# Message products of two batches at once by Strassen's form, with block sums made by accumulating DMAs

## The chip, the cores and the metric

The kernel runs on one core of a Trainium2 chip. The metric is device time in microseconds (us) of that core; lower is better. Five engines run side by side, each through its own list of instructions in order: TensorE (PE, matmuls into PSUM), VectorE (DVE), ScalarE (ACT), GpSimd (POOL) and SyncE (SP, which only issues DMAs). An engine whose next instruction must wait holds up everything behind it in its own list.

## The reference

Two layers work on `x` of 16 batches x 1024 nodes x 128 features with one symmetric 0/1 matrix `adj` of 1024 x 1024.

```python
x = layernorm(x + attention(x, adj))      # layer 0, once per batch
h = x                                     # layer 1: five steps of a gated unit
for _ in range(5):
    m  = adj @ h                          # the message product; m_in and m_out are the same here
    z  = sigmoid([m, m] @ w3.T + b3 + h @ u3.T + c3)
    r  = sigmoid([m, m] @ w4.T + b4 + h @ u3.T + c3)
    hv = tanh([m, m] @ w5.T + b5 + (r * h) @ u5.T + c5)
    h  = (1 - z) * h + z * hv
out = layernorm(x + h)
```

Because both adjacency inputs are `adj`, `[m, m] @ w.T` is `m @ (wa + wb).T`; the kernel adds the two halves of each weight once. The tests of the inputs that let the kernel use a short form of the softmax end in a flag; a slower general program stands behind it and is not run here.

## The kernel before

**Data.** `h` is kept in two layouts: `hT` (features on the 128 partitions, 1024 nodes along them) for the gates, and, as weights of the message product, `hN` (nodes on partitions, in 8 chunks of 128). `adj` stays in SBUF as `float32r`[...]; the weights side is split into two `float32r` numbers (high part and rest, `split`, L501 and following) so that two matmuls give the product of a float32 by a 0/1 matrix. A message product of one batch and one step is therefore 2 halves of the nodes x 8 chunks x 2 parts = 32 matmuls of 128 x 512 (L895). The gates (L926, L936, L952, L953) use plain float32 matmuls, ten per batch and step.

**One step of one batch.** The 32 message matmuls go into two PSUM banks; ScalarE copies each to `m` (L913). For each half: `h @ u3` (L926), copied by ScalarE into a second bank (L929) so that both gates can add onto it, two gate matmuls (L936), two tanh (L939), `r*h` on VectorE (L946), two matmuls (L952, L953), tanh (L956), three VectorE instructions that write `hT` (L963, L970, L977). Then the new `h` is turned into `hN`: VectorE transposes 32 x 32 blocks (`T`, L494), four DMAs write the result to a DRAM tile `D` with the blocks in swapped places (L499), one DMA reads it back (`F`, L503), ScalarE writes the high part (L513) and VectorE the rest (L517).

**Layer 0** of each batch (`layer0`) has 32 more matmuls of the same kind (L766), some float32 ones, softmax sums on VectorE, two such turns through DRAM and a layernorm whose power is taken on GpSimd (L463 to L466).

**The order.** Nothing is scheduled by hand. `Plan` takes every piece of work with an engine, a length, a rank and what it reads and writes, plays the engines forward with these lengths and assumed delays, and at each free engine takes the ready piece of lowest rank; buffers have to be free. The instructions are emitted in that order. `rank_of(b, s)` is `5*b + 3*s`, so some three batches are in flight at once, and the last three are spread out to end together. `D` holds offsets from that rank for each kind of work. The delay that the planner assumes between a turned block's read and its use is 2.3 us after the issue.

**DMA queues.** SP issues all DMAs but four of the start. Each of the DMA semaphores is waited for before it is used again; a read of `D` waits on SP for the four writes to land.

Of the kernel before, what the change touches and what calls it, by code (L numbers as in the profile page):

```python
# [26 lines left out]
TINY = 1e-30  # L27
IDLE = 24
# [101 lines left out]
def kernel(  # L130
# [51 lines left out]

# [15 lines left out]
    b5 = const.tile([P, 1], F32, tag="b5", name="b5")  # L198
    ident = const.tile([P, P], F32, tag="ident", name="ident")
# [3 lines left out]
    zeros = const.tile([P, HALF], F32, tag="zeros", name="zeros")  # L203
# [7 lines left out]
    def exact(pools):  # L211

        def pool(name, bufs, space=None):
# [4 lines left out]
        adj = table.tile([P, NC, N], F32R, tag="adj", name="adj")  # L218
        cnt = table.tile([P, NC], F32, tag="cnt", name="cnt")
# [5 lines left out]
            "hl": (2, [P, 2, NC, P], F32R, None),  # L225
            "yT": (1, [P, N], F32, None),
            "part": (1, [P, HALF], F32, None),
            "junk": (1, [P, HALF], F32, None),
            "y0": (4, [P, NC, P], F32, None),
            "hN": (4, [P, 2, NC, P], F32R, None),  # L230
            "hT": (4, [P, N], F32, None),
            "T": (3, [P, HALF], F32, None),
            "F": (3, [P, HALF], F32, None),
            "m": (4, [P, HALF], F32, None),
# [3 lines left out]
            "o": (2, [P, NC, P], F32, None),  # L238
            "look": (2, [P, HALF], F32, None),
# [9 lines left out]
            "D": (6, [P, HALF], F32, bass.MemoryType.DRAM),  # L249
            "ud": (2, [3, N], F32, bass.MemoryType.DRAM),  # L250
# [42 lines left out]
        D = dict(m=0, pu=0, u=0, pr=0.2, pz=0.2, sr=0.3, r=0.3, pv=0.4, sz=0.5, z=0.5, hv=0.6, h=0.6, tr=0.6, split=0.8)  # L293
        D.update(o=3, ln=3.5, out=4, l1=-7, l2=-6, l3=-5, l4=-4, l5=-3, l6=-2.5, l7=-2, l8=-1)

# [3 lines left out]

        def rank_of(b, s):  # L300

            if b < B - 3:
                return 5 * b + 3 * s
            begin = 5 * b - 2 * (b - B + 3)
            end = 5 * B + 4 - 2 * (B - 1 - b)
            return begin + (end - begin) * s / 4


        boot = ("hl", "boot")
        cols = {"wot": slice(0, 128), "a": slice(128, 130), "ws": slice(256, 384), "w345": slice(384, 1152)}  # L310

        def W(name):
            return T(boot, F32, [P, 2 * N])[:, cols[name]]

        ws = ("T", "ws")
        staged = [("hN", "boot", k) for k in range(NC // 2)]
        x0 = ("xt", 0)

        def adj_half(k, e):
            hs = slice(e * HALF, (e + 1) * HALF)  # L320
            rows = adj_t[2 * k * P : 2 * (k + 1) * P, hs].rearrange("(c p) n -> p c n", p=P)
            return T(staged[k], F32, [P, 2, N])[:, :, hs], rows

        def early_loads():
# [28 lines left out]
            writes=[(boot, "early"), (ws, "early"), (x0, "early"), (("xt", 1), "early"), *((t, "early") for t in staged)],  # L353
# [7 lines left out]
        lands(8, [(staged[0], 0)])  # L361
        lands(1, [(("wo",), 0)])
        for k in range(1, NC // 2):
            lands(8, [(staged[k], 0)])
        for k in range(NC // 2):
            lands(8, [(staged[k], 1)])
# [3 lines left out]
        def constants():  # L370
            make_identity(nc, ident)
            nc.gpsimd.memset(shift, -SHIFT)
            nc.gpsimd.memset(ones, 1.0)
            nc.gpsimd.memset(mhalf, -0.5)
            nc.gpsimd.memset(zeros, 0.0)
# [31 lines left out]
        def fill_(k):  # L407
            nc.tensor.matmul(T(("gz", "fill", k)), ident, zeros, start=True, stop=True)
# [10 lines left out]
        def sums():  # L419
            w = W("w345").rearrange("p (j t e) -> p j t e", j=3, t=2)  # L420
            nc.vector.tensor_tensor(wm, w[:, :, 0, :], w[:, :, 1, :], ALU.add)
            nc.vector.tensor_tensor(b5, bias[:, 2:3], bias[:, 4:5], ALU.add)
            nc.vector.tensor_scalar(u5h, u5, 0.5, None, ALU.mult)
# [10 lines left out]
        def adj_tables(c):  # L434
            st = staged[c // 2]

            def left(copy):
                copy(adj[:, c, 0:HALF], T(st)[:, c % 2, 0:HALF])

            def right():  # L440
                nc.scalar.activation(
                    adj[:, c, HALF:N], T(st)[:, c % 2, HALF:N], AF.Identity, accum_out=cnt[:, c : c + 1]
                )

            if c < 4:
                dve(420, -60, lambda: left(nc.vector.tensor_copy), reads=[(st, 0)], writes=[(("A",), c, 0)])
            else:
                act(A, -60, lambda: left(nc.scalar.copy), reads=[(st, 0)], writes=[(("A",), c, 0)])
            act(640, -50, right, reads=[(st, 1)], writes=[(("A",), c, 1)])


        def layernorm(key, g, rank, after, src, dst, write):
# [8 lines left out]
            def power():  # L461
# [3 lines left out]
                nc.gpsimd.tensor_scalar(r[:, 1, :], mean, -1.0, None, ALU.mult)  # L465
                nc.gpsimd.tensor_tensor(r[:, 1, :], r[:, 1, :], r[:, 0, :], ALU.mult)  # L466
# [21 lines left out]
        def flip(name, src, read, dst, write, rank):  # L488


            t, d = ("T", *name), ("D", *name)

            def turn():
                nc.vector.transpose(T(t).rearrange("p (b c i) -> p b c i", b=4, c=4), turned(src()))  # L494

            def away():
                swapped = T(d).rearrange("(b i) (a x) -> a i b x", b=4, a=4)
# [3 lines left out]
            dve(V, rank, turn, reads=read, writes=[(t, 0)])  # L501
            sp(1830, rank, away, reads=[(t, 0)], writes=[(d, 0)], lag=1500)
            sp(450, rank, lambda: nc.sync.dma_start(dst(), T(d)), reads=[(d, 0)], writes=[write], lag=2300)  # L503

        def split(b, s, g, src, read, rank):

            n = ("hN", b, s)
            gs = slice(4 * g, 4 * g + 4)

            def half(k):  # L510
                return T(n)[:, k, gs, :].rearrange("p c (a j) -> p c a j", a=4)

            act(A, rank, lambda: nc.scalar.copy(half(0), src()), reads=read, writes=[(n, g, 0)])  # L513
# [4 lines left out]
                reads=[*read, (n, g, 0)],  # L518
                writes=[(n, g, 1)],
            )  # L520


        def layer0(b):

            first = rank_of(b, 0) - (60 if b == 0 else 0)
# [4 lines left out]
            q, zs, rz, yT, y0, hT = ("q", b), ("zs", b), ("rz", b), ("yT", b), ("y0", b), ("hT", b)  # L530
# [3 lines left out]
            for g in range(4):  # L534
                ph = ("ps", "g", b, "ph", g)

                def ph_(g=g, ph=ph):
                    for j in range(2):
# [13 lines left out]
                pe(460, rank, ph_, reads=[(xt, g // 2), (("wo",), 1)], writes=[(ph, 0)])  # L552
# [135 lines left out]
            rank = rank_of(b, 0) + D["l2"]  # L688
            junk = ("junk", b)
            for c in range(NC):  # L690

                st = staged[c // 2]

                def z_(c=c, st=st):
                    nc.vector.scalar_tensor_tensor(  # L695
                        T(junk),
                        T(st)[:, c % 2, 0:HALF] if b == 0 else adj[:, c, 0:HALF].bitcast(F32),
# [36 lines left out]
            rank = rank_of(b, 0) + D["l3"]  # L734
            size = 1 if b == 0 else 4
            for w in range(2):
                hl = ("hl", b, w)
                for c0 in range(0, NC, size):
                    cs = range(c0, c0 + size)

                    def hi_(w=w, cs=cs, hl=hl):
                        for c in cs:
                            nc.scalar.activation(
                                T(hl)[:, 0, c, :], T(hx)[:, c, 0:P], AF.Copy, scale=T(rz)[:, w, c : c + 1]
                            )

                    def lo_(w=w, cs=cs, hl=hl):
                        for c in cs:
                            nc.vector.scalar_tensor_tensor(  # L749
                                T(hl)[:, 1, c, :],  # L750
                                T(hx)[:, c, 0:P],
                                T(rz)[:, w, c : c + 1],
                                T(hl)[:, 0, c, :].bitcast(F32),
# [5 lines left out]
                    act(1250 * size / 4, rank, hi_, reads=r, writes=[(hl, c, 0) for c in cs])  # L759
                    dve(1050 * size / 4, rank, lo_, reads=[*r, *((hl, c, 0) for c in cs)], writes=[(hl, c, 1) for c in cs])  # L760

            def product(po, w, cs, hs, first, last):
                hl = T(("hl", b, w))
                terms = [(k, c) for c in cs for k in range(2)]
                for i, (k, c) in enumerate(terms):
                    nc.tensor.matmul(  # L766
                        T(po),
                        hl[:, k, c, :],
                        adj[:, c, hs],
                        start=(first and i == 0),  # L770
                        stop=(last and i == len(terms) - 1),
                    )

            rank = rank_of(b, 0) + D["l4"]
            left = slice(0, HALF)
            right = slice(HALF, N)
            for g in range(2):
                po = ("ps", "acc", b, "po", g)
                part = (yT, "p") if g == 0 else (("part", b), "p")

                def part_(g=g, po=po, part=part):
                    dst = T(yT)[:, left] if g == 0 else T(part[0])
                    nc.vector.tensor_tensor(dst, T(po), pairs()[:, g, :], ALU.mult)

                for c0 in range(4 * g, 4 * g + 4, size):
                    cs = range(c0, c0 + size)

                    def po_(g=g, po=po, cs=cs):
                        product(po, 0, cs, left, cs[0] == 4 * g, cs[-1] == 4 * g + 3)
# [5 lines left out]
                        reads=[*((("hl", b, 0), c, k) for c in cs for k in range(2)), *((("A",), c, 0) for c in cs)],  # L795
# [4 lines left out]
            def add_():  # L800
                nc.vector.tensor_tensor(T(yT)[:, left], T(yT)[:, left], T(("part", b)), ALU.add)

            dve(V, rank, add_, reads=[(yT, "p"), (("part", b), "p")], writes=[(yT, "s")])
# [5 lines left out]
                reads=[(xt, 0), (("wsi",), 0)],  # L809
# [5 lines left out]
                lambda: nc.vector.tensor_tensor(T(yT)[:, left], T(px), T(yT)[:, left], ALU.add),  # L815
# [541 lines left out]
```

## Time and profile before

| | |
|---|---|
| Median of 3 runs | 1521.95 us (1521.3 to 1523.5) |
| The profiled execution | 1525.58 us, its span 1523.8 us |
| PE busy | 1496.8 us (98%), 5204 instructions |
| PE weight loads busy | 947.5 us (62%) |
| DVE busy | 988.6 us (65%) |
| ACT busy | 824.4 us (54%) |
| POOL busy | 146.3 us (10%) |
| DMA on the main queue | 142.78 MB, 32.9% of the 16 engines' time |
| Granted TensorE clock | 0.99 of full |

The span runs from the first to the last instruction; 1.8 us of the profiled execution lie outside it. "Busy" is the union of an engine's instructions; matmuls overlap in the pipeline, so the mean length of one in a group is longer than the distance between two. "Idle before" names what an engine waited for. The chain is followed back from the last instruction to whatever released it, so the time that it gives to a line is time in which nothing else bounded the end.

### The profile page before, as it was taken

What the parts mean: (1) busy time and instruction counts of PE and PEld (TensorE: products, weight loads), DVE (VectorE), ACT (ScalarE), POOL (GpSimd) and SP (SyncE); (2) the same over time, 40 slices, a digit from 0 to 9 for tenths busy, and PEclk for the clock granted to TensorE, in tenths of its full rate; (3) what the DMA queues carried; (4) which work ended last, traced back from release to release, by engine and by line L of the source; (5) the groups of instructions that cost most, each with busy time, mean ns of one, the idle gap of its engine ahead of it and who ended that gap; (6) DMA issues with size and microseconds to landing.
All of it is one profiled execution on the core that took longest, in us unless ns stands there. A gap on an engine that the chain in (4) does not pass through costs nothing.

```text
span 1523.8 us, 17516 instructions
## 1 busy us (share of the span) xinstructions
PE 1496.8 (98%) x5204; PEld 947.5 (62%) x5204; DVE 988.6 (65%) x2438; ACT 824.4 (54%) x1656; POOL 146.3 (10%) x266
## 2 busy tenths in 40 slices
PE   9889999999999999999999999999999999999996
PEld 7556666666666666666666666666666665656663
DVE  6565777667666666766666666765768775454554
ACT  5454645565554555645565554555656546444454
POOL 0100011011110101111011110101111011010011
PEclk9889999999999999999999999999999999999998
DMA  4013445242433324334232433424343433223121
GB/s 172 24 43 113 117 137 148 73 124 78 129 85 97 108 62 125 88 105 117 77 113 82 125 84 97 112 61 119 91 118 94 115 86 95 83 68 85 56 62 37
DMA packets 193980, 144.82 MB, mean 95 GB/s; under 512 B 33279, under 2 KB 158934, under 8 KB 193878
## 3 DMA queue, kind: packets, MB, share of 16 engines
q1 hardware_dynamic: 193314, 142.78, 32.9%
q8 instruction: 42, 0.69, 0.2%
q10 hardware_dynamic: 564, 0.85, 0.2%
q14 instruction: 60, 0.49, 0.1%
HBM read 79.95 MB, written 63.61 MB: 94 GB/s over the span
## 4 chain that ended last, share of the span: by engine, by line
PE 95%; DMA 2%; DVE 1%; POOL 1%; ACT 0%; SPq 0%; issue 0%; POOLq 0%
PE ps_acc L895 39%; PE gz L936 9%; PE ps_g_r L936 9%; PE ps_g_r L926 9%; PE ps_g_v L953 9%; PE ps_g_v L952 9%; PE ps_acc_po L766 7%; PE ps_g_ph L540 1%; PE ps_acc_px L808 1%; PE ps_acc_po L822 1%; DMA hN_boot<-in_adj_dram 1%; DMA hl_boot<-in_L_gnn_w_w_dram 1%; DMA D<-T 0%; DVE junk L695 0%; ACT y L471 0%
## 5 line engine op out<-in xcount | busy, mean ns | idle before, releaser
L895 PE MATMUL ps_acc<-adj,hN 128*128 128x512 f32 x2560 | 682.0, 419 | 1.5 <-ACT y L471 1.5
L895 PEld LDWEIGHTS ps_acc<-adj,hN 128*128 128x128 f32 x2560 | 483.5, 189 | 174.2 <-issue 59.5
L913 ACT COPY m<-ps_acc 128x512 f32<-128x512 f32 x160 | 93.3, 583 | 250.6 <-PE ps_acc L895 249.9
L946 DVE SCALAR_TENSOR_TENSOR r<-r,hT 128x512 f32<-128x512 f32 x160 | 109.3, 685 | 116.4 <-ACT r L939 115.9
L963 DVE TENSOR_TENSOR hv<-hv,hT 128x512 f32<-128x512 f32 x160 | 108.8, 684 | 101.6 <-ACT hv L956 101.2
L956 ACT ACTIVATE hv<-ps_g_v,b 128x512 f32<-128x512 f32 x160 | 108.8, 684 | 104.3 <-PE ps_g_v L953 104.0
L953 PE MATMUL ps_g_v<-r,u5h 128*128 128x512 f32 x320 | 163.5, 592 | 0.0
L952 PE MATMUL ps_g_v<-m,wm 128*128 128x512 f32 x320 | 163.4, 592 | 0.0
L936 PE MATMUL gz<-m,wm 128*128 128x512 f32 x320 | 163.4, 592 | 0.0
L936 PE MATMUL ps_g_r<-m,wm 128*128 128x512 f32 x320 | 163.4, 592 | 0.0
L517 DVE TENSOR_TENSOR hN<-F,hN 128x512 fp32r<-128x512 f32 x128 | 87.8, 687 | 110.4 <-ACT hN L513 109.9
L926 PE MATMUL ps_g_r<-hT,u 128*128 128x512 f32 x320 | 151.7, 595 | 0.7 <-ACT hT L878 0.7
L766 PE MATMUL ps_acc_po<-adj,hl 128*128 128x512 f32 x512 | 138.3, 420 | 0.4 <-DVE hl L749 0.3
L939 ACT ACTIVATE r<-ps_g_r,bh 128x512 f32<-128x512 f32 x160 | 110.1, 688 | 39.9 <-PE ps_g_r L936 39.5
L766 PEld LDWEIGHTS ps_acc_po<-adj,hl 128*128 128x128 f32 x512 | 96.1, 188 | 36.4 <-issue 14.6
L939 ACT ACTIVATE z<-gz,bh 128x512 f32<-128x512 f32 x160 | 107.6, 686 | 11.7 <-PE gz L936 11.3
L929 ACT COPY gz<-ps_g_r 128x512 f32<-128x512 f32 x160 | 90.8, 571 | 35.7 <-PE ps_g_r L926 34.7
L977 DVE SCALAR_TENSOR_TENSOR hT<-hv,hT 128x512 f32<-128x512 f32 x160 | 107.2, 676 | 3.5 <-PE ps_g_r L926 0.5
L970 DVE SCALAR_TENSOR_TENSOR hv<-z,hv 128x512 f32<-128x512 f32 x160 | 108.0, 680 | 1.8
L953 PEld LDWEIGHTS ps_g_v<-r,u5h 128*128 128x128 f32 x320 | 60.7, 190 | 76.9 <-issue 63.6
L936 PEld LDWEIGHTS gz<-m,wm 128*128 128x128 f32 x320 | 60.8, 190 | 76.6 <-issue 76.6
L494 DVE STREAM_TRANSPOSE T<-hT 128x512 f32<-128x512 f32 x154 | 107.1, 702 | 1.9 <-DMA D_b<-T_b 1.2
(134 smaller groups left out, 1298.4 us busy)
## 6 DMA issues: line engine op xcount, KB each, us to landing
D<-T SPq DMA_DIRECT2D x616, 64.0 KB
F<-D SPq DMA_DIRECT2D x154, 256.0 KB
out_dram<-o SPq DMA_DIRECT2D x32, 256.0 KB
xt<-in_x_dram SPq DMA_DIRECT2D x15, 512.0 KB
pb<-ud SPq DMA_DIRECT2D x14, 512.0 KB
D_y<-T_y SPq DMA_DIRECT2D x112, 64.0 KB
F_y<-D_y SPq DMA_DIRECT2D x28, 256.0 KB
D_b<-T_b SPq DMA_DIRECT2D x112, 64.0 KB
```

The source lines that it names most:

```text
L766: nc.tensor.matmul(T(po), hl[:, k, c, :], adj[:, c, hs], start=(first and i == 0), stop=(last and i == len(terms) - 1),)
L895: nc.tensor.matmul(T(pm), T(hN)[:, k, c, :], adj[:, c, hs[e]], start=(c == 0 and k == 0), stop=(c == NC - 1 and k == 1),)
L926: nc.tensor.matmul(T(pr), u3, h(), start=True, stop=True)
L936: nc.tensor.matmul(T(p_), wm[:, j, :], T(m), start=False, stop=True, skip_group_check=True)
L939: nc.scalar.activation(T(t), T(p_), AF.Tanh, bias=bh[:, j : j + 1], scale=0.5)
L946: lambda r=r, h=h: nc.vector.scalar_tensor_tensor(T(r), T(r), 1.0, h(), ALU.add, ALU.mult),
L952: nc.tensor.matmul(T(pv), wm[:, 2, :], T(m), start=True, stop=False)
L953: nc.tensor.matmul(T(pv), u5h, T(r), start=False, stop=True)
L956: nc.scalar.activation(T(hv), T(pv), AF.Tanh, bias=b5, scale=1.0)
L963: lambda hv=hv, h=h: nc.vector.tensor_tensor(T(hv), T(hv), h(), ALU.subtract),
L970: lambda hv=hv, z=z: nc.vector.scalar_tensor_tensor(T(hv), T(z), 1.0, T(hv), ALU.add, ALU.mult),
L977: lambda hv=hv, h=h: nc.vector.scalar_tensor_tensor(h(), T(hv), 0.5, h(), ALU.mult, ALU.add),
```

## The change

Two batches `one = 2q` and `two = 2q+1` go through each step together. `h` of each is cut in two along the nodes (g = 0, 1), and `adj` in four quarters Y11, Y12, Y21, Y22. Instead of eight products of a half `h` by a quarter of `adj` (8 matmuls each), seven are made:

- four sums of quarters, `tab` T1 to T4, are made once on VectorE (`sums_of_adj`);
- the sums of `h` blocks are made in DRAM: `leave` writes the turned `h` to DRAM tiles `X`, and `add_to` issues a DMA from GpSimd that adds one DRAM tile to another. Four such additions per pair and step, each reading what the one before wrote or overwriting what it read: X(two,1) += X(two,0); X(two,0) += X(one,0); X(one,0) += X(two,1); X(one,1) += X(one,0);
- seven reads bring blocks x11, x12, x22 (before a sum) and s1, s3, s2, s4 (after the sums) to SBUF, where each is split into two `float32r` parts as before;
- products go into banks a, b, c; partial sums are copied out of a bank by ScalarE while the next product is added onto what stays there, and two VectorE instructions add or subtract bank c.

The batch with even number is carried with its sign turned (`sign`), so that all sums are additions. Six of the forty pair-steps, listed in `PLAIN`, keep eight products. Ranks are by pair, `10*(b//2) + 4.5*s`; the offsets `D` are new; `y0` no longer stays in SBUF but is written to DRAM (`yd`) and read back at the end; buffers change in number (`blk` takes the place of `hl` and `hN`); the matmuls that fill the `gz` banks at the start use the identity and not a tile of zeros.

```diff
+PLAIN = {(0, 0), (0, 1), (0, 2), (7, 2), (7, 3), (7, 4)}
...
-            "hl": (2, [P, 2, NC, P], F32R, None),
-            "y0": (4, [P, NC, P], F32, None),
-            "hN": (4, [P, 2, NC, P], F32R, None),
-            "hT": (4, [P, N], F32, None),
+            "blk": (8, [P, 2, NC // 2, P], F32R, None),
+            "y0": (2, [P, NC // 2, P], F32, None),
+            "hT": (6, [P, N], F32, None),
...
+            "X": (24, [P, HALF + 16], F32, bass.MemoryType.DRAM),
+            "yd": (24, [P, HALF], F32, bass.MemoryType.DRAM),
...
-        D = dict(m=0, pu=0, u=0, pr=0.2, pz=0.2, sr=0.3, r=0.3, pv=0.4, sz=0.5, z=0.5, hv=0.6, h=0.6, tr=0.6, split=0.8)
+        D = dict(m=-0.4, pu=0.8, u=0, pr=0.0, pz=0.2, r=-0.3, pv=0.0, z=0.5, hv=0.4, h=0.6, tr=1.0, o=3.4, ln=3.5)
...
         def rank_of(b, s):
-            if b < B - 3:
-                return 5 * b + 3 * s
-            begin = 5 * b - 2 * (b - B + 3)
-            end = 5 * B + 4 - 2 * (B - 1 - b)
-            return begin + (end - begin) * s / 4
+            return 10 * (b // 2) + 4.5 * s
...
+            def t13():
+                nc.vector.tensor_tensor(T1(c), f(Y11), f(Y12), ALU.subtract)
+                nc.vector.tensor_tensor(T3(c), f(Y22), f(Y12), ALU.subtract)
+            def t24():
+                nc.vector.scalar_tensor_tensor(T2(c), f(T1), -1.0, f(Y22), ALU.mult, ALU.subtract)
+                nc.vector.scalar_tensor_tensor(T4(c), f(T2), -1.0, f(Y21), ALU.mult, ALU.subtract)
...
+        def add_to(d, other, rank):
+            plan.add(
+                "POOL",
+                1000,
+                rank,
+                lambda: nc.gpsimd.dma_start(T(d)[:, 0:HALF], T(other)[:, 0:HALF], accum_op=ALU.add),
+                reads=[(other, 0), (d, 0)],
+                writes=[(d, 0)],
+                lag=3500,
+            )
...
+        def messages(q, s, k):
...
+            from_dram(one, 1, blk["x12"])
+            from_dram(one, 0, blk["x11"])
+            from_dram(two, 1, blk["x22"])
+            add_to(X(two, 1), X(two, 0), rank)
+            from_dram(two, 1, blk["s1"])
+            add_to(X(two, 0), X(one, 0), rank)
+            add_to(X(one, 0), X(two, 1), rank)
+            from_dram(one, 0, blk["s2"])
+            from_dram(two, 0, blk["s3"])
+            add_to(X(one, 1), X(one, 0), rank)
+            from_dram(one, 1, blk["s4"], True)
...
+            multiply(a, blk["x11"], Y11, y(0, 0), True, True)
+            copy(b, "part", a)
+            multiply(b, blk["x12"], Y21, y(1, 0), False, True, [(b, "part")])
+            copy(m[one, 0], 0, b)
+            multiply(c, blk["s1"], T1, t, True, True)
+            multiply(a, blk["s2"], T2, t, False, True)
+            copy(m[one, 1], "part", a)
+            multiply(a, blk["s3"], T3, t, False, True)
+            copy(m[two, 1], "part", a, -1)
+            combine(m[two, 1], c, ALU.subtract)
+            multiply(a, blk["x22"], T4, t, False, True)
+            copy(m[two, 0], 0, a, -1)
+            multiply(c, blk["s4"], Y22, y(1, 1), False, True)
+            combine(m[one, 1], c, ALU.add)
```

Here `from_dram` is one DMA read of 256 KB issued by SP and the split behind it; `multiply` is eight matmuls of one block (4 chunks x 2 parts) by a quarter or a sum of quarters; `copy` is one ScalarE instruction out of a bank and `combine` one VectorE instruction.

## The prediction

> **What bounds the kernel now.** I read the page from the top: busy times, slices, then the chain that ended last.
>
> ```profile
> span 1523.8 us, 17516 instructions
> PE 1496.8 (98%) x5204; PEld 947.5 (62%) x5204; DVE 988.6 (65%) x2438; ACT 824.4 (54%) x1656; POOL 146.3 (10%) x266
> ...
> PEclk9889999999999999999999999999999999999998
> ...
> q1 hardware_dynamic: 193314, 142.78, 32.9%
> ...
> PE 95%; DMA 2%; DVE 1%; POOL 1%; ACT 0%; SPq 0%; issue 0%; POOLq 0%
> ```
>
> TensorE carries 95% of the chain at full clock, so a microsecond of matmul less is a microsecond less until something else ends last. The groups and the stages say what else is near:
>
> ```profile
> L895 PE MATMUL ps_acc<-adj,hN 128*128 128x512 f32 x2560 | 682.0, 419 | 1.5 <-ACT y L471 1.5
> L895 PEld LDWEIGHTS ps_acc<-adj,hN 128*128 128x128 f32 x2560 | 483.5, 189 | 174.2 <-issue 59.5
> ...
> L517 DVE TENSOR_TENSOR hN<-F,hN 128x512 fp32r<-128x512 f32 x128 | 87.8, 687 | 110.4 <-ACT hN L513 109.9
> ```
>
> ```profile
> 400.00:1200.00 800.00, 800.00 (x2762) 506.05 (x2761) 537.06 (x1337) 450.48 (x912) 89.74 (x152) 1.00 0.35 99
> ```
>
> In this stage (columns PE, weight loads, DVE, ACT, POOL, clock, DMA share) PE has no gap in 800 us; DVE is at 67%, ACT at 56%. The mean of 419 ns overlaps in the pipeline. The distance between matmuls comes from the chain in order of time, near the end:
>
> ```profile
> 1493.42 3.73 PE ps_acc L895 x16
> ...
> 1506.05 0.87 PE ps_g_v L953 x2
> ```
>
> So a message matmul R costs 3.73/16 = 0.233 us and a float32 matmul F 0.86. A load of weights (189 ns) stays under R. For the turn through DRAM I read SP's and ACT's instructions in order of time:
>
> ```profile
> 827.16 1.77 SPq L499 DMA_DIRECT2D D<-T  x4
> 830.27 0.34 SPq L503 DMA_DIRECT2D F<-D  x1
> ```
>
> ```profile
> 782.22 0.34 SPq L503 DMA_DIRECT2D F<-D  x1
> ...
> 784.95 0.62 ACT L513 CAST hN<-F 128x512 fp32r<-128x512 f32 x1 [0.79 <-DMA F<-D]
> ```
>
> Four writes: 3.1 us from the first issue until the read may go. The read: 784.95 - 782.22 = 2.75 us until ScalarE starts.
>
> **What the Trainium skill says.** "DMA: Bandwidth & Descriptors", section "SWDGE vs HWDGE vs iDMA": an accumulating DMA can only be issued from GpSimd, which computes the descriptors in software. The trace of before has no such DMA. Same page, "Anatomy of one DMA — SWDGE (gpsimd) path": about 2.0 us + bytes/436e3, most of it the receipt of the last write. 256 KB gives 2.6; the trace's SP-issued read took 2.75, which agrees. Same page, "Rules for kernel authors": an accumulate reads its destination and writes later, so the next DMA on these bytes must wait for its semaphore; no run here shows it, but it means that the four additions stand in series.
>
> **The change part by part.**
>
> *Matmuls removed.* 34 pair-steps of 40 make 56 instead of 64: 34 x 8 = 272 x 0.233 = **-63.4 us**. The gates keep their 800 F. The built program has 2800 matmuls of the R kind against 3072.
>
> *ScalarE.* Casts 262 against 160 (+102 x 0.617, row L513 = 63 us); copies out of banks 194 against 160 (+34 x 0.583, row L913 = 20). 824 + 83 = 907 us, 61% of 1475. *VectorE.* +102 subtractions at 0.687 (70), 68 combines of a bank and an SBUF tile (row L783, 0.68: 46), 16 sums of adj (11): 1116 us, 76%. In the stage 400 to 1200: a pair-step adds five VectorE instructions, 3.4 us; some 21 pair-steps stand there (1481 us of matmuls over 40 is 37 each), so (537 + 71)/(800 - 39) = 80%. Both hide under PE as totals; the cover gets thin and costs some tenths where a gate waits behind a subtraction.
>
> *SP.* Reads +130, `yd`, `o` and `X` +92: 222 issues x 0.34 = 75 us beside some 490, no bound. But 136 reads wait on SP for an addition; behind them stand the other pair's writes of `X`, which then start late. *POOL.* 136 DMAs, about four per 37 us, between layernorm powers (about 2.5 us each). *DMA engines.* By bytes: 58 MB more in plain transfers, 36 MB in additions, moved up to three times; 33% becomes 55 to 75%. Not full, but latencies may grow.
>
> *The new chain.* From the end of batch two's last gate matmul: tanh 0.7 + 0.2, three VectorE 2.1 + 0.2, transpose 0.7 + 0.1, four writes 3.1 + 0.1: X is written at +7.2; read of x22 until +9.9. Then additions of L each: s1, s3, s2, s4 can be cast at 12.7 + L, + 2L, + 3L, + 4L, and multiplied 1.6 us later. L is not in the trace. Lower bound 2.75 (a plain read of the same size); upper: the skill's formula with three times the bytes, 2.0 + 1.8, and the 1 us that its section "Latency and other measured facts" gives to GpSimd's emission, 4.8, and under load perhaps a third more, 6.5. I take 4.2; the planner laid the order out for 4.5, which is no evidence.
>
> What cover is there? I counted, in the order of the built program, the PE work between that last gate matmul and each product, with R and F as above. Among the 27 pair-steps after a first step, s2 has at least 30.2 us and s4 at least 38.4: limits L = (30.2 - 14.3)/3 = 5.3 and (38.4 - 14.3)/4 = 6.0. ScalarE is stricter: a late cast holds the tanh behind it. Example, batches 10 and 11, step 2: behind s4's cast stands the copy L1102 of a PE result that is due at +33.1; so L may be (33.1 - 0.6 - 12.7)/4 = 4.9. Over the 27, the least limit of the four blocks runs from 4.4 (quarter 5.4, half 5.9, three quarters 6.7) up to 9. With L above the limit a pair-step loses links x (L - limit); summed over all: L = 5: 2 us; 5.5: 13; 6: 35; 6.5: 66; 7: 107. At 4.2: **0**.
>
> *Bank a used four times running.* s2, copy, s3: only one F stands between in the built order, 0.86, against a copy of 0.58 with about 0.2 us to each side, 0.98. 34 x 0.2 with queueing on ACT = **+7**.
>
> *End.* Pair 7 runs steps 2 to 4 with eight products and, once pair 6 has ended, alone. From batch 14's half 0 to its next product needs 0.9 + 2.3 + 0.8 + 3.2 + 2.75 + 1.5 = 11.4 us; the order puts there one half of batch 14's and all of batch 15's last matmuls, 10 F = 8.6. About 3 us lost, twice, and some tenths for the last tanh: **+7**. Before, the last three batches were spread and PE had no gap from 100 to 1508 us.
>
> *Start.* The memset of `zeros` (1.9 us of PE's wait) goes; batch 1's layernorm is now covered by batch 0's gates (4.3 + 1.5 us of waits on L471 gone); but batches 0 and 1 come to step 2 with 7.8 us of PE work where 11.4 are needed, and the tables of adj sit on VectorE: **0**, between -6 and +6.
>
> Sum, on the profiled execution: 1525.6 - 63.4 + 7 + 7 = 1476.2. The median of the runs is 3.6 us under the profiled time: **1473**.
>
> **The rivals.**
>
> *VectorE and ScalarE queues.* At 80% the r chain (tanh 0.69, L946 0.69, then L953) has 2.6 to 3.4 us of cover in the order; if each of the 136 halves loses 0.3 us behind a subtraction, 41 us go: 1473 + 41 = 1514, or 1495 with half of it. For: DVE already waits 110 us for ACT at L517, the kind of instruction that is added. Against: at 67% PE lost nothing.
>
> *The additions become the bound (slower).* Place: `add_to` on GpSimd, in series, then SP's and ScalarE's in-order queues. It decides where the losses of the list above reach 49 us, at L = 6.3; at L = 7 it gives 1473 + 107 = 1580. For: DRAM to DRAM with three times the traffic on engines at twice the load; descriptor emission in software, GpSimd's layernorm powers in between. Against: the upper price of 4.8.
>
> *It doesn't do what it says.* If PE were held by weight loads, fewer matmuls would still be fewer loads; if the removed time only turns into waits at the same places, no change. Little speaks for it.
>
> **How the numbers follow.** Forecast case (1457 to 1488) 0.57; queues (1488 to 1519) 0.21; no change 0.03; additions too slow 0.19. The bound of a measured difference here is about 0.2%, 3 us. Faster 0.78, same 0.03, slower 0.19. Low end: no losses at all, 1525.6 - 63.4 - 3.6 = 1459, and the best start, less 3: 1456. High end 1525 leaves about 0.17 above and 0.02 below. Range of the forecast case alone: 1457 to 1488.
>
> **What would show it.** Right: 2800 R matmuls at the same distance; PE still above 90% of the chain; POOL-issued adds that land in 3.5 to 5 us (SP's waits of its reads on the DMA X<-X short); ScalarE's waits on reads of F_x near none; gaps in PE of 3 us only in the last 90 us. Wrong: PE gaps in the middle stages released by ACT casts of blk_s (additions) or by L1119 (queues); DVE over 83% there; DMA share above 70%. What would make the prediction wrong is L first, then the start.

## The result, and the profile after

The changed kernel takes **1597.86 us** (median of 4 runs, 1592.2 to 1603.78) against 1522.72 for the kernel before, measured beside it: a ratio of 1.0495, 95% interval 1.0454 to 1.0536. It is 5% slower; 1473 was forecast, and 1525 was the upper end of the range. The profiled execution took 1596.28 us. From its page, the lines that answer to those of before: span, busy times, granted clock in 40 slices, DMA queues.

```profile
span 1594.5 us, 18201 instructions
PE 1478.0 (93%) x4932; PEld 908.5 (57%) x4932; DVE 1094.1 (69%) x2625; ACT 891.5 (56%) x1792; POOL 260.1 (16%) x401
...
PEclk9999999999999999999999999999999999999997
...
q1 hardware_dynamic: 225282, 200.99, 43.2%
q0 software_dynamic: 19584, 35.66, 15.9%
```

PE has 272 matmul instructions fewer, but its busy time fell by 18.8 us where 63.4 were taken out, and it stands idle for 1594.5 - 1478.0 = 116.5 us where it was 27.0. The span moved by 89.5 - 18.8 = 70.7 us. The gaps are everywhere. Stages, with the columns PE, weight loads, DVE, ACT, POOL, granted clock, DMA share, GB/s:

```profile
100.00:400.00 300.00, 279.06 (x936) 173.47 (x934) 222.67 (x561) 166.40 (x344) 47.56 (x72) 0.97 0.64 167
400.00:1200.00 800.00, 754.41 (x2471) 459.07 (x2472) 570.30 (x1348) 465.59 (x936) 147.09 (x213) 0.98 0.67 165
1200.00:1480.00 280.00, 266.75 (x838) 160.05 (x837) 174.08 (x357) 154.81 (x283) 45.12 (x71) 0.98 0.58 141
1480.00:1600.00 120.00, 87.04 (x259) 50.07 (x257) 49.78 (x107) 47.93 (x84) 10.38 (x20) 0.87 0.21 58
```

In the middle stage PE had no gap before; now 45.6 of 800 us. VectorE is *less* full there than was forecast (71%, not 80%), because the stage runs slower; DMA is at 0.67 where it was 0.35. Who waits for whom (us in total, times, longest), first SP's queue, then ScalarE, then PE:

```profile
SPq L547 <- DMA X<-X: 418.6, 113, 7.9
```

```profile
ACT blk_s L571 <- DMA F_x_s<-X: 198.2, 87, 8.4
```

```profile
PE ps_g_r L1109 <- ACT gz L1102: 22.1, 13, 5.2
PE ps_acc_a L583 <- ACT m L1052: 13.3, 9, 3.7
PE ps_g_v L1126 <- DVE r L1119: 12.5, 10, 3.0
```

SP waits 419 us for additions, ScalarE 198 us for the reads behind them, and PE for ScalarE instructions (the copy of the gate bank, L1102) that stand behind such casts in ScalarE's list. The additions themselves, GpSimd's list in order of time (start, duration, in brackets the wait):

```profile
715.18 0.81 POOL L559 DMA_DIRECT2D X<-X  x1 [4.19 <-DMA X<-T]
719.66 0.81 POOL L559 DMA_DIRECT2D X<-X  x1 [3.67 <-DMA X<-X]
725.09 0.81 POOL L559 DMA_DIRECT2D X<-X  x1 [4.63 <-DMA X<-X]
```

One starts some 4.5 to 5.4 us after the other. All this looks like the rival "the additions become the bound". Yet by the working of the prediction a link of 5 us would have cost 2 us, 5.5 us 13, and not 125, if the chain had started when it was forecast to. So the waits are what one sees; whether they are the cause is for the experiments. (The chain that ended last, which carried the reading of the kernel before, can't be used: in this trace it stops 9 us before the end.)

### The profile page after: what moved, and what is told of

Read it like the earlier page. It is cut to its first block, busy times and chain, and to the rows that moved or that the text cites. A ratio compares the mean times of both kernels' runs of the same rounds, so it can differ in the third digit from the quotient of the medians.

```text
span 1594.5 us, 18201 instructions
## 1 busy us (share of the span) xinstructions
PE 1478.0 (93%) x4932; PEld 908.5 (57%) x4932; DVE 1094.1 (69%) x2625; ACT 891.5 (56%) x1792; POOL 260.1 (16%) x401
## 3 DMA queue, kind: packets, MB, share of 16 engines
q1 hardware_dynamic: 225282, 200.99, 43.2%
q0 software_dynamic: 19584, 35.66, 15.9%
## 5 line engine op out<-in xcount | busy, mean ns | idle before, releaser
L559 POOL DMA_DIRECT2D X<-X x136 | 114.3, 840 | 891.2 <-DMA X<-X 310.5
L571 ACT CAST blk_s<-F_x_s 128x512 fp32r<-128x512 f32 x136 | 83.6, 619 | 201.9 <-DMA F_x_s<-X 198.2
L583 PE MATMUL ps_acc_a<-tab,blk_s 128*128 128x512 f32 x544 | 156.9, 430 | 17.6 <-ACT m L1052 13.3
L575 DVE TENSOR_TENSOR blk_s<-F_x_s,blk_s 128x512 fp32r<-128x512 f32 x136 | 92.6, 684 | 83.8 <-ACT blk_s L571 83.5
L583 PE MATMUL ps_acc_po<-adj,blk 128*128 128x512 f32 x512 | 145.5, 429 | 0.0
L583 PEld LDWEIGHTS ps_acc_a<-tab,blk_s 128*128 128x128 f32 x544 | 105.4, 198 | 62.4 <-ACT m L1052 22.3
L583 PEld LDWEIGHTS ps_acc_po<-adj,blk 128*128 128x128 f32 x512 | 96.1, 188 | 40.3 <-issue 17.3
L583 PE MATMUL ps_acc<-adj,blk_h 128*128 128x512 f32 x384 | 104.3, 431 | 14.2 <-ACT blk_h L571 8.6
L1109 PEld LDWEIGHTS ps_g_r<-m,wm 128*128 128x128 f32 x320 | 59.9, 193 | 90.7 <-issue 45.6
```

What stands on the lines that cost most here:

```text
L559: lambda: nc.gpsimd.dma_start(T(d)[:, 0:HALF], T(other)[:, 0:HALF], accum_op=ALU.add),
L583: nc.tensor.matmul(T(bank), T(blk)[:, k, c, :], right(c), start=(first and i == 0), stop=(last and i == len(terms) - 1), skip_group_check= ...
L1109: nc.tensor.matmul(T(p_), wm[:, j, :], T(m), start=False, stop=True, skip_group_check=True)
```

## The experiments

Three theories were laid down before the first runs. **A**: the waits on the additions, in series and through the in-order lists of SP and ScalarE. **B**: VectorE and ScalarE have too much in their lists. **C**: the additions load the DMA engines, and all other transfers come late. Each run was timed against the kernel before on its chip (1521 to 1522 us there). How long a transfer took is worked out from the trace: from SP's issue to the last increment of its semaphore, over 100 to 1480 us.

### The additions left out

```diff
-                lambda: nc.gpsimd.dma_start(T(d)[:, 0:HALF], T(other)[:, 0:HALF], accum_op=ALU.add),
+                lambda: None,
```

> The changed kernel with its 136 additions left out: GpSimd issues none, every other instruction stands in the same place on its engine, and the reads for s1 to s4 bring h blocks that were never summed, so the messages are wrong. Late additions (A: they stand in series at some 5 us each, and SP's and ScalarE's lists wait behind them): the time falls to 1470 to 1500 us, SP's waits on them vanish, PE's idle falls from 116 us to under 50. Vector and scalar load (B: 5 more VectorE and 4 more ScalarE instructions per pair-step): nothing of that is taken away, it stays above 1570. DMA traffic (C: the engines are 60 to 70% busy and every read is slower): as A, since 16 points of the traffic go too.

**1504.78 us**, ratio 0.9882 [0.9866, 0.9899]. The order of all other work is the same, and so is VectorE's and ScalarE's load. In the middle stage PE is nearly full again, at DVE 77% and ACT 64%:

```profile
400.00:1200.00 800.00, 795.32 (x2664) 489.68 (x2663) 615.52 (x1458) 509.29 (x1013) 84.28 (x144) 1.00 0.52 149
```

A and C expected at most 1500 us and under 50 us of PE's idle time; 57 us are left. Theory B is out as the main cost: the longer lists of VectorE and ScalarE leave a gain. 93 us of the result hang on the additions.

### The additions made aside

The same 136 DMAs at the same places of GpSimd's list and in the same series, but on four scratch tiles `Z` (filled with zeros at the start) that nobody reads.

```diff
+            aside = {(False, 1): (0, 1), (False, 0): (1, 2), (True, 0): (2, 0), (True, 1): (3, 2)}[one, d[3]]
-                lambda: nc.gpsimd.dma_start(T(d)[:, 0:HALF], T(other)[:, 0:HALF], accum_op=ALU.add),
+                lambda: nc.gpsimd.dma_start(
+                    T(("Z", aside[0]))[:, 0:HALF], T(("Z", aside[1]))[:, 0:HALF], accum_op=ALU.add
+                ),
```

> The same additions at the same places on GpSimd, in the same series, but on four scratch tiles of zeros that nothing else reads; the messages are wrong, as in the run without additions. A: no read waits for them, so 1475 to 1505, near the run without them. C: the traffic is all there, so near 1590, and the reads stay slow. B: above 1570.

**1571.36 us** (1559.65 to 1579.58), ratio 1.0329 [1.0266, 1.0393]. Nothing waits for an addition any more, and 66 of the 93 us stay. The middle stage:

```profile
400.00:1200.00 800.00, 766.03 (x2538) 470.16 (x2537) 587.01 (x1393) 481.83 (x967) 149.21 (x222) 0.99 0.69 169
```

The four writes that turn `h` now land 2.60 us after their issue (median; 4.76 for the slowest tenth) where they took 1.82 (3.28) without additions; the reads of summed blocks took 3.33 for 2.98. That is theory C, or else GpSimd's list: the layernorm's power stands there too, behind additions that wait for each other. One thing is not as in the changed kernel: nothing holds the additions back, so the first of four is issued some 3 us before the tanh of batch two (median), and not 14.3 us after it. So their load meets other transfers: in the changed kernel the writes take as long as here (2.59 us), but the reads of summed blocks took 2.74.

### An eighth of the rows, aside and in place

Two kernels part these: the additions aside over 16 of 128 rows (same issues, same series, an eighth of the load), and the real additions on `X`, with all their waits, over 16 rows.

```diff
-T(("Z", aside[0]))[:, 0:HALF], T(("Z", aside[1]))[:, 0:HALF]
+T(("Z", aside[0]))[0:16, 0:HALF], T(("Z", aside[1]))[0:16, 0:HALF]
```

> The additions go aside onto scratch tiles that nobody reads, in the same places of GpSimd's list and in the same series, but over 16 of 128 rows: as many issues and waits on GpSimd, an eighth of the descriptors and bytes. The sums of h are left out. Without any additions the kernel took 1505 us, with whole additions aside 1571. Theory C (the additions' load on the DMA engines slows the writes and reads that the chain waits for): 1507 to 1518, and the median write of X, 1.82 us without additions and 2.60 with them, falls to about 1.9. Rival Q (additions stand in GpSimd's list, each waits for the one before, and the layernorm powers behind them come late): an addition keeps most of its fixed time, so 1545 to 1571.

**1505.77 us**, 0.9899 [0.988, 0.9919].

```diff
-                lambda: nc.gpsimd.dma_start(T(d)[:, 0:HALF], T(other)[:, 0:HALF], accum_op=ALU.add),
+                lambda: nc.gpsimd.dma_start(T(d)[0:16, 0:HALF], T(other)[0:16, 0:HALF], accum_op=ALU.add),
```

> The real additions on the tiles of h, with every wait on them, over 16 of 128 rows; seven eighths of the sums are left out. Theory C, load: the time falls from 1598 to about 1515 to 1535, since what is left is the series of fixed DMA times (a link of 4 to 4.5 us in place of 5). Rival A (the series of waits itself is the cost): a link stays near 4.5 to 5 and the time at 1560 to 1595.

**1504.03 us**, 0.9887 [0.9868, 0.9906]: as without any addition. From its page (line of the software queue) and its list of DMA issues (KB each, median us from issue to landing):

```profile
q0 software_dynamic: 4352, 4.47, 2.3%
```

```profile
X<-X POOLq DMA_DIRECT2D x136, 32.0 KB, 2.7
```

Both came out below every range that was laid down for them, so what is left beside the load is less than was thought. GpSimd's list costs nothing: ScalarE waited 28.6 us for layernorm powers with whole additions aside and 27.1 us without any. The series of four waits costs nothing either while a link is short: it took 3.1 us here and 5.1 in the changed kernel (from first to fourth addition, by three; median over the 27 pair-steps after a first step). s4 was cast 35.4 us after the tanh of batch two, 40.1 in the changed kernel, and 35.9 without any addition. So 35 to 36 us is where ScalarE's list comes to this cast when it waits for nothing. The run over 16 rows takes away the load and the long links at once; long links on unloaded engines were not tried.

### Copies in place of additions, once and twice

Is it that a DMA accumulates, or that it keeps the engines busy? First the DMAs aside copy and do not add; then there are two such copies for each addition, in two series on eight scratch tiles.

```diff
-T(("Z", aside[1]))[:, 0:HALF], accum_op=ALU.add
+T(("Z", aside[1]))[:, 0:HALF]
```

> As the run with whole additions aside (1571 us), but each DMA copies and does not accumulate: the same rows, issued from GpSimd in the same series; the sums of h are left out. If the load counts by bytes moved and descriptors, copying costs two thirds of it or more: 1545 to 1571. If accumulating itself is what disturbs the other transfers, the time falls to 1505 to 1525.

**1526.29 us**, 1.0037 [1.0025, 1.005]: between the two ranges, 1 us above the lower one.

```diff
+                lambda: [
+                    nc.gpsimd.dma_start(T(("Z", aside[0] + k))[:, 0:HALF], T(("Z", aside[1] + k))[:, 0:HALF])
+                    for k in (0, 4)
+                ],
```

> As the run with copies aside (1526 us; 8.4% of the DMA engines' time on GpSimd's queue), but two copies in place of each addition, in two series of their own, so that they take the engines for as long as the additions did (16.6%); the sums of h are left out. If it is the share of the DMA engines' time that delays the other transfers, it comes to where the additions aside were: 1555 to 1580, and the median write of X goes from 2.27 us to about 2.6. If accumulating is worse than the time that it takes of the engines, it stays at 1530 to 1548.

**1572.99 us**, 1.036 [1.0309, 1.041]. The software queue of the additions aside, of one copy and of two copies:

```profile
q0 software_dynamic: 20096, 36.71, 16.6%
```

```profile
q0 software_dynamic: 11392, 36.71, 8.4%
```

```profile
q0 software_dynamic: 22784, 73.42, 15.6%
```

The same bytes cost half the engine time when they are copied: copies went as 4 KB packets of 159 ns, additions as 2 KB packets of 178 ns (medians), while a plain 2 KB packet of a read took 84. Two copies take about the time of one addition and cost the same 66 to 68 us. So neither the bytes nor accumulating as such counts, but the share of the engines' time, or the number of packets, which goes along with it here (20096, 11392 and 22784); these two no run parts. GpSimd waited about as long for its DMAs with one copy (307 us) as with two (323), so its list does not explain the 47 us between them. The series in one table, the kernels with the changed kernel's order of work (X writes: median, and slowest tenth above; half clock: see below):

| kernel | us | software queue | X writes, us | PE idle, us | half clock, us |
|---|---|---|---|---|---|
| no additions | 1505 | none | 1.82, 3.28 | 57 | 41 |
| real, 16 rows | 1504 | 2.3% | 1.94, 3.30 | 58 | 38 |
| one copy aside | 1526 | 8.4% | 2.27, 3.96 | 73 | 41 |
| additions aside | 1571 | 16.6% | 2.60, 4.76 | 102 | 65 |
| two copies aside | 1573 | 15.6% | 2.63, 4.76 | 106 | 75 |
| the changed kernel | 1598 | 15.9% | 2.59, 4.92 | 117 | 82 |

It fits what the Trainium skill says in "DMA: Bandwidth & Descriptors", section "Queues, rings and completion order": each DMA engine takes its queues in turn, a packet at a time. The trace agrees in its effect (the main queue's transfers lengthen while the engines are at 0.69 and not full); the turns themselves no run shows.

### A longer lag for the planner

```diff
-                lag=3500,
+                lag=4200,
```

> One number: the planner is told that an addition lands 4.2 us after its issue and not 3.5 (5.2 with the issue, where the trace of the changed kernel shows 4.8 to landing and 5.0 from one addition to the next). Another order comes of it, the same work. A: what waits in the wrong place moves, 1500 to 1560. B and C: 1585 to 1605, no difference.

**1590.50 us**, 1.0463 [1.0443, 1.0483]. An order made for a link of 5.2 us is at best 7 us better, which is not clear of noise (the two intervals overlap), and lies where B and C put it. SP waits less on additions (286 us for 419), but the time hardly moves.

### No Strassen at all

All 40 pair-steps with eight products: what remains of the change is work by pairs, new ranks, `yd`, the buffers.

```diff
-PLAIN = {(0, 0), (0, 1), (0, 2), (7, 2), (7, 3), (7, 4)}
+PLAIN = {(q, s) for q in range(8) for s in range(5)}
```

> All forty pair-steps with eight products: no additions, no combines, four reads and splits per pair-step as before the change; pairs, ranks, y0 through DRAM and the buffers stay as changed. A, B and C all: 1525 to 1550 (nothing saved, some us lost at the end where one pair is alone). If the pairing, the new ranks or y0's way are the cost themselves, 1590 or more.

**1551.77 us**, 1.0198 [1.0181, 1.0215]. It is 2 us above the range. The rest of the change loses 30 us against the kernel before. Of the span's 25.5 us, 20 are gaps of PE (13 of them between 100 and 1480 us, 11 more in the tail after that, 4 fewer in the first 100) and 5 are busy time. Strassen without the load takes off 47 of the possible 63.

### The load on the kernel before

The kernel before in its own order, with one addition aside at each of 136 copies of a gate bank.

```diff
-                def u_(pr=pr, pz=pz):
+                def u_(pr=pr, pz=pz, e=e):
                     nc.scalar.copy(T(pz), T(pr))
+                    if (b // 2, s) not in ((0, 0), (0, 1), (0, 2), (7, 2), (7, 3), (7, 4)):
+                        i, j = ((0, 1), (1, 2), (2, 0), (3, 2))[2 * (b % 2) + e]
+                        nc.gpsimd.dma_start(T(("Z", i))[:, 0:HALF], T(("Z", j))[:, 0:HALF], accum_op=ALU.add)
```

> The kernel before, with nothing changed in the order of its work, but 136 additions of 256 KB aside onto scratch tiles, in one series from GpSimd, one at each of 136 copies of the gate bank. It tells what the load alone costs a kernel whose TensorE had no gaps. If the load costs the same everywhere: +45 to +66 us, so 1567 to 1588. If it costs only where the turn through DRAM had no slack: 0 to +15, 1522 to 1537, with writes of D at 2.4 us and more for 1.80 and PE still at 97% or 98%.

**1546.69 us**, 1.0144 [1.011, 1.0179]: +25 us, between what the two views gave, so both missed. Writes of `D` went from 1.80 (slowest tenth 2.35) to 1.87 (3.93), those of layer 0's `D_b` from 1.83 to 3.91 in the median. The middle stage here, and in the run with real additions over 16 rows:

```profile
400.00:1200.00 800.00, 792.62 (x2715) 497.68 (x2714) 528.08 (x1310) 434.45 (x890) 155.04 (x229) 1.00 0.55 126
```

```profile
400.00:1200.00 800.00, 795.68 (x2674) 491.29 (x2674) 615.52 (x1459) 510.86 (x1015) 154.93 (x236) 1.00 0.55 153
```

The engines' total share is the same, 0.55, but the run over 16 rows lost nothing against the same kernel without additions. So the total share alone does not set the cost. Why the load costs 25 us here and 66 there stays open: the kernel before may have more slack in its turn, the engines' total is lower (0.55 for 0.69), and part of the 25 may be GpSimd's list, since ScalarE waited 56 us for layernorm powers here and 35 before.

### The sums in SBUF

If the load is the cause, sums that never touch DRAM should win. Four blocks are read per pair-step, in place of seven, and tile is added to tile in place; `F` has 8 buffers, `blk` 6, and the planner assumes 2.0 us for writes (it was 1.5) and 2.9 for reads (2.3).

```diff
-                lambda: nc.gpsimd.dma_start(T(d)[:, 0:HALF], T(other)[:, 0:HALF], accum_op=ALU.add),
+                lambda: nc.gpsimd.tensor_tensor(T(d), T(d), T(other), ALU.add),
...
+            for to, other, name in (
+                ((two, 1), (two, 0), "s1"),
+                ((two, 0), (one, 0), "s3"),
+                ((one, 0), (two, 1), "s2"),
+                ((one, 1), (one, 0), "s4"),
+            ):
+                add_to(f[to], f[other], rank)
+                cast(f[to], blk[name], name == "s4")
```

> The sums of h are made in SBUF: four reads per pair-step in place of seven, and GpSimd adds one tile of 128x512 to another in place (136 additions), then the same casts. F has 8 buffers for 4, blk 6 for 8; the planner assumes 2.9 us for reads and 2.0 for writes. If the load on the DMA engines and the DRAM series are what costs the change its gain, this is below the kernel before: 1490 to 1515, with X writes near 1.9 us. If GpSimd's addition is slow (over 3 us) or holds VectorE up, or the chain of casts itself is the bound, it stays above: 1525 to 1570.

**1541.33 us**, 1.0138 [1.0121, 1.0155]. X writes are back at 1.80 us, yet it is slower than the kernel before. The groups of GpSimd's additions and of VectorE's subtractions that follow them:

```profile
L558 POOL TENSOR_TENSOR F_x<-F_x,F_x 128x512 f32<-128x512 f32 x136 | 202.1, 1486 | 615.4 <-DVE blk_x L573 562.4 <-ACT blk L814 25.4 <-DMA X<-T 20.2
L573 DVE TENSOR_TENSOR blk_s<-F_x,blk_s 128x512 fp32r<-128x512 f32 x136 | 107.6, 805 | 11.6 <-ACT blk_s L569 8.7 <-POOL rstd_o L500 2.5 <-ACT o L508 0.2
```

An addition on GpSimd takes 1.49 us, and a VectorE subtraction 805 ns where it took 684 in the changed kernel; VectorE's busy time grew by 96 us though it got no work. PE waits 26.9 us for `r` from VectorE. Then the same additions on VectorE:

```diff
-                "POOL",
-                1200,
+                "DVE",
+                605,
                 rank,
-                lambda: nc.gpsimd.tensor_tensor(T(d), T(d), T(other), ALU.add),
+                lambda: nc.vector.tensor_tensor(T(d), T(d), T(other), ALU.add),
```

> As the run with sums in SBUF (1541 us), but VectorE makes them and not GpSimd, whose additions took 1.49 us each and beside which VectorE's subtractions took 0.805 us in place of 0.687. If GpSimd lengthened VectorE's work[...], VectorE's busy time comes out as before (1190 us: 136 x 0.687 = 93 more than 1096, in place of 95 lost), the additions are 0.8 us shorter each, and the time is 1525 to 1545. If the length of the chain had been the bound, 1500 to 1520.

**1522.29 us**, 1.001 [0.9998, 1.0022]: as the kernel before, 19 us better than on GpSimd, and between the two ranges that were laid down. The addition takes 682 ns and the subtraction is back at 684, so VectorE does the additions for less (1168 us busy) than it lost beside GpSimd (1190).

### The sums on VectorE, planned for their load

In that kernel the planner's allowance of 1.2 on VectorE's and ScalarE's lengths makes VectorE look almost full in its plan. Here the allowance is 1.1, and the turn of `h` gets an earlier rank.

```diff
-    MARGIN = 1.2
+    MARGIN = 1.1
...
-        D = dict(m=-0.4, pu=0.8, u=0, pr=0.0, pz=0.2, r=-0.3, pv=0.0, z=0.5, hv=0.4, h=0.6, tr=1.0, o=3.4, ln=3.5)
+        D = dict(m=-0.4, pu=0.8, u=0, pr=0.0, pz=0.2, r=-0.3, pv=0.0, z=0.5, hv=0.4, h=0.6, tr=0.6, o=3.4, ln=3.5)
```

> As the run with the sums on VectorE (1522 us), with the order laid out for its own load: the planner's allowance on VectorE's and ScalarE's lengths falls from 1.2 to 1.1 of the estimate (at 1.2 its plan shows VectorE as nearly full), and the turn of h is ranked 0.6 after its step and not 1.0. If the gaps that the run with VectorE's sums still shows (PE idle 69 us) are a matter of order: 1495 to 1515, below the kernel before. If VectorE at 83% of the middle stage is the bound whatever the order: 1518 to 1535.

**1495.92 us** (1495.41 to 1498.25), ratio 0.9833 [0.982, 0.9847]: faster than both kernels. Page and middle stage:

```profile
PE 1443.6 (97%) x4932; PEld 898.7 (60%) x4932; DVE 1172.2 (78%) x2761; ACT 901.2 (60%) x1792; POOL 144.8 (10%) x265
```

```profile
400.00:1200.00 800.00, 796.87 (x2690) 493.85 (x2689) 678.35 (x1579) 516.18 (x1031) 78.52 (x144) 1.00 0.45 128
```

VectorE is at 85% in this stage and PE has 3 us of gaps. So the seven products are worth having with the sums on VectorE and an order made for that. Of the 102 us between this kernel and the changed one, 76 came with the place of the sums, four reads in place of seven and the planner's longer delays, and 26 with the allowance and the rank together; nothing parts them further, and the changed kernel was never planned with these settings.

## Why the prediction was wrong

The forecast of 1473 and the measured 1598 lie 125 us apart. By the runs: 32 without any addition (1505), 66 more when the additions load the engines aside (1571), 27 more when they are waited for (1598). The runs of the additions aside spread by 20 us, so the last two are good to some 10. Nor are they two separate causes: aside, the load falls at other moments, and ScalarE waits 198 us for summed blocks in the changed kernel, 53 with the additions aside and 31 without any.

**The step that failed: "DMA engines ... Not full, but latencies may grow", with no price.** The share was forecast at 55 to 75% and came to 59.6% (43.2 + 15.9, with 0.5 of the small queues), 64 to 67% in the loaded stages. I treated engines that are not full as free. But with the additions' load, waited for or not, the writes that turn `h` land 0.8 us later in the median and 1.6 in the slowest tenth, and the load alone cost 66 us. The way from there to PE is read from the waits and not tested by itself: with the additions aside PE waits 27.5 us for ScalarE's gate copies (L1102 in the changed kernel), without them 5.9; the copies stand behind casts of late blocks.

**The length of the chain.** Its parts after the tanh of batch two, predicted and measured (medians of the 27 pair-steps):

| | predicted | measured |
|---|---|---|
| X written, read of x22 issued | +7.2 | +10.7 |
| first addition issued | +9.9 | +14.3 |
| a link, first to fourth addition by three | 4.2 | 5.1 |
| s4 cast | +29.5 | +40.1 |

The link was in its bounds (2.75 to 6.5), and the prediction's upper price of 4.8 would have been nearer than the 4.2 that I took. What failed is the start of the chain: the first addition came 4.4 us later than the sum said. Most of that is not load: over 16 rows it came at +13.6, and without any addition x22's read was issued at +10.1. The sum took each piece of work as started when its data were there, and left out the lists and queues that it stands in. With a start 4.4 us later and a link of 5.1, s4 comes as late as the list has it for L = 5.1 + 4.4/4 = 6.2, and that costs some 47 us by the list (an estimate from the prediction's own figures). Over 16 rows the same sum gives 3.1 + 3.7/4 = 4.0 and no loss, as measured. So the runs do not refute the list of losses; it was entered at the wrong place. The rival "the additions become the bound" pointed the right way, but its point, L = 6.3, holds for the forecast start alone. (By its own two lines the read that was taken as 2.75 us took 2.73; nothing hangs on that.)

**TensorE's clock, not priced at all.** 63.4 us of matmuls were removed; PE's busy time fell by 18.8. The trace knows a full and a half clock. PE's instructions in order of time show what a gap does:

```profile
306.36 3.41 PE L1109 MATMUL ps_g_r<-m,wm 128*128 128x512 f32 x4 [3.19 <-ACT gz L1102]
309.61 1.88 PE L1109 MATMUL gz<-m,wm 128*128 128x512 f32 x4
```

After 3.19 us of waiting, four matmuls take 3.41 us, and the next four, of the same kind, 1.88. The Trainium skill describes this in "TensorE: Matmul & The Clock Gate", section "What's actually happening": the clock is at half or full, set by the activity in windows of about 3.4 us. The trace agrees: it has these two clocks alone, and up to the last one at the end its half-clock stretches last 3.4 or 6.8 us (10.2 in the kernel before). There are 20 of them, 82 us, against 2 and 20 before; 61 us more at half speed is up to 31 us of the 44.6 that the matmuls should have saved. It takes less than a gap of 3 us. Here the gap is 1.90 us; then the stretch that follows it, with the granted clock in the third column from the end:

```profile
1335.60 2.90 PE L583 MATMUL gz<-adj,blk_x 128*128 128x512 f32 x8 [1.90 <-ACT gz L1052]
```

```profile
1336.70:1340.10 3.40, 3.40 (x8) 1.97 (x7) 3.40 (x7) 1.12 (x3) 0.00 (x0) 0.50 0.70 166
```

Of the 20 stretches 5 follow a gap of over 3 us; before the other 15 the longest gap was 1.9 to 2.9 us, and PE was idle for about half of the last 3.4 us or more. Not every such gap did it: one of 2.76 us at 1079 us did not. So a gap of 2 us can cost well over its own length.

**Start, bank a and end: gaps of 14 us predicted, 30 measured.** The span of the run without additions, 1507.1, lies 46.7 us above 1523.8 - 63.4: 30 us of gaps and 17 of busy time. The gaps beside those of before: -4 in the first 100 us, +16 to 400, +5 to 1200, +14 from there on. The end (+7) and the start (0, at most +6) were too small; bank a's +7 has room for at most 5 in the middle stage. Of the 17 us of busy time, half-clock stretches (41 us for 20) explain 10; the rest stays open.

**The queue rival.** ScalarE's 891 us and VectorE's 1094 came out near 907 and 1116. The run without additions carries them with 5 us of gaps in the middle stage: the steps on these two engines held, and the rival is not the cause. **SP** was "no bound". With 16 rows it still waits 153 us on additions, at 1504, so waits of that size cost nothing; what the 419 us of the changed kernel cost by themselves no run shows.

**The chances.** 0.19 for slower was too little: the forecast case gave every new transfer a length that was taken from a kernel at about half the DMA load (0.35 for 0.67 in the middle stage).

## What to carry to other kernels

A transfer that nobody waits for is not free: on a kernel whose loop turns through DRAM, price added DMA work by the engine time that it takes (its packets times the measured time of one; an accumulating DMA took about twice that of a plain one for its bytes) and by what it does to the transfers that are waited for. In this kernel family 8.4% more of the engines' time cost 21 us and 16% cost 66 to 68; on the kernel before 16.9% cost 25, so the price has to be measured where it is to be used. Before adding up lengths from the trace of before, ask which of them were measured at a load that the change itself alters, add the wait in each in-order list that a piece of work stands in, and give TensorE's gaps of 2 us and more a price of more than their length. If a sum can be made on tiles that already lie in SBUF, try it on the engine that has room, and give the planner the true lengths.

## What the runs showed of the hardware

- An accumulating DRAM-to-DRAM DMA of 256 KB from GpSimd lands 4.8 us after its issue in the changed kernel (median; 3.6 to 7.0), one of 32 KB after 2.7, a plain copy of 256 KB after 3.7, each in the kernel of its own run. GpSimd spends 0.84 us on issuing the accumulating one and 0.55 on the copy.
- Accumulating moved 35.66 MB in 15.9% of the engines' time, where 200.99 MB of plain transfers took 43.2%: about twice as much per byte.
- Load can leave the median of other transfers and lengthen the slow ones: in the kernel before with additions aside, the median write of `D` lengthened by 0.07 us and the slowest tenth by 1.6. Layer 0's writes of `D_b` there lengthened by 2.1 us in the median.
- In the changed kernel TensorE's granted clock fell to half after gaps of 1.9 us and more, for 3.4 or 6.8 us at a time.
- A GpSimd addition of two 128x512 float32 tiles takes 1.49 us, VectorE's 0.68, and beside it VectorE's own subtractions lengthen by 18%.
